# Ordering two off-path steps of a convolution by the scans that run beside it

## The chip, the cores and the metric

The kernel runs on one NeuronCore of one Trainium2 chip. The metric is device time in microseconds (us) of one launch, from its first to its last instruction, as the median of several runs. Engines are named as in the profile: PE is TensorE (PEld its weight loads), DVE is VectorE, ACT is ScalarE, POOL is GpSimd, SP is SyncE, which here only issues DMAs.

## The reference

Four layers run on `x` of shape (4, 128, 64, 64). Only the first two bear on this change; they run together in one function, `layers01`. The other two (linear attention with an expert layer, then windowed attention with an expert layer) follow it and are not touched.

```python
# layer 0, for each image: a selective scan over L = 4096 tokens, 256 channels, 16 states
delta = softplus(dt_r @ dt_proj_w.T + dt_proj_b)
def step(hprev, inp):
    dt_t, B_t, C_t, x_t = inp
    hn = exp(dt_t[:, :, None] * A) * hprev + (dt_t * x_t)[:, :, None] * B_t[:, None, :]
    return hn, einsum('bdn,bn->bd', hn, C_t)

# layer 1, for each image: a hypergraph convolution over the 4096 tokens
incidence = (dist < 16.0)                       # (4096, 4096) zeros and ones
xe = xf @ W_fc.T + b_fc
edge = einsum('bve,bvc->bec', incidence, xe) / deg_e
vert = einsum('bve,bec->bvc', incidence, edge) / deg_v
out = vert + xf
mean, var = over images and tokens, for each channel   # then a batch norm and silu
```

## The kernel before

**Two layers beside each other.** `layer0()` is a generator that yields after every half state. A state is one of the 16 scan states of one chunk of 512 tokens; an image has 8 chunks, so 128 states or 256 half states. `layer1(b, ...)` is a second generator for the convolution of image `b`. The driver first runs image 0 of layer 0 alone and 12 half states of image 1. Then for each of three images it takes 256 half states of layer 0, and after each lets `layer1` go on until the share of its work (costs `W_CMP`, `W_TURN`, `W_EDGE`, `W_VERT` and so on) has caught up. The fourth image of layer 1 runs alone. A counter `tick` grows by one with each half state (in the fourth image, with each yield of `layer1`).

**A state on the engines.** SP loads the rows of B and C, `bt` (L287). POOL makes `db` = `dx` times B (L291, two buffers). ACT makes the decays `hs` with two exponentials (L303, in PSUM, two buffers). DVE scans each half (L309), saves the carry (L318) and multiplies by C into `ho` (L319). In images 1 to 3 POOL adds eight `ho` up (L324, L326) before PE adds the sums in PSUM.

**The convolution.** In the panel phase, PE makes distances (L541) which DVE compares into the 0/1 matrix `inc` (L544); half of the blocks are transposes of others instead (PE L553, ACT L557). `edges` adds up each block of 128 edges with 32 matmuls (L564). Two ticks later `parts` takes the sum on DVE (`ed`, L571), and after the fourth block of a chunk DVE makes the reciprocal degrees `rdeg` (L575, L576), POOL multiplies `ed` by them (L580), ACT copies the product to fp16 as `hi` (L581) and POOL takes the rest `lo` (L582), both in the tensor `es`. In the vertex phase, for each of 8 chunks, PE adds 64 matmuls of `es` and `inc` into `ps_v` (L672). Then `mean` scales the result on DVE (L680, into `rb`, which ACT had filled with the reciprocal degrees of the vertices, L667) and adds the input on POOL (L681); `finish` takes batch statistics on DVE (L684) and stores `rb` by a DMA on SP's queue (L685). The tile `rb` has two buffers, `ps` in PSUM has four.

**What sets the order.** A step that must not come too early is queued by `later(k, f)` and called by `due()` once `tick` has grown by `k`; `due(True)` calls everything at once. `due(True)` runs ahead of the first `edges` of each chunk, and the last chunk's steps are flushed before the vertex phase.

```python
due()
later(1, mean)
later(6, finish)
```

The order in which instructions are written is only a preference. The compiler plans each engine's queue by its own estimate of durations: of the instructions that it takes to be ready, the one written first goes next. So an instruction can be placed ahead of others that were written before it, when the plan thinks the engine idle. Instructions that pass through `act()` are the exception: each gets an order edge to the one before, so ACT's queue here is exactly as written. Once planned, each queue runs in order.

Of the kernel before, what the change touches and what calls it, by code (L numbers as in the profile page):

```python
# [12 lines left out]
ALU = mybir.AluOpType  # L13
# [18 lines left out]
def bc(ap, n):  # L32

    return ap.unsqueeze(1).to_broadcast([ap.shape[0], n, ap.shape[1]])


def bc_last(ap, n):

    return ap.unsqueeze(len(ap.shape)).to_broadcast([*ap.shape, n])


class Net:
# [36 lines left out]
    def layers01(self):  # L79
        nc, tc, a = self.nc, self.tc, self.a  # L80
# [10 lines left out]
        with ExitStack() as ctx:  # L91
# [90 lines left out]
            late = ctx.enter_context(tc.tile_pool(name="late", bufs=1))  # L182


            order = []

            def act(i):


                if order:  # L190
                    tc.add_manual_dep(
                        i.ins, order[-1].name,
                        mybir.DependencyInfo(mybir.DependencyClass.NoSync, mybir.DependencyReason.DATA),
                        reason="order",
                    )
                order[:] = [i.ins]


# [3 lines left out]
            def later(k, f):  # L202
                waiting.append((self.tick + k, f))

            def due(every=False):
                for w in list(waiting):
                    if every or w[0] <= self.tick:
                        waiting.remove(w)
                        w[1]()

            def before(b, c):
# [21 lines left out]
                def conv():  # L233
                    xc = s["xc"] = w2.tile([P, 2, T], F32, tag="xc", name="xc")
                    for h in range(2):
                        act(nc.scalar.activation(xc[:, h, :], s["ps"][h], AF.Silu, bias=vec[:, h, 4:5]))
# [56 lines left out]
            def state(s, n, h):  # L293

                b, c, db = s["b"], s["c"], s["db", n]
                if h == 0:
                    hs = s["hs"] = aps.tile([P, 2, T], F32, tag="hs", name="hs")  # L300
                    s["ho", n] = w2.tile([P, 2, T], F32, tag="ho", name="ho", bufs=6)
                    for k in range(2):
                        act(nc.scalar.activation(hs[:, k, :], s["dl"][:, k, :], AF.Exp, scale=A[:, k, n : n + 1]))  # L303
                hs, ho = s["hs"], s["ho", n]
                ct = bc(s["bt", n][:, 1, :], 2)
                split = b == 0 and n in TO_POOL
                init = 0.0 if c == 0 else carry[:, n, h : h + 1]
                to = ho if split else hs
                nc.vector.tensor_tensor_scan(to[:, h, :], hs[:, h, :], db[:, h, :], init, ALU.mult, ALU.add)  # L309
                if h == 0:  # L310
                    return
                if split:
                    if c < NT - 1:
                        nc.gpsimd.tensor_copy(carry[:, n, :], ho[:, :, T - 1])
                    nc.gpsimd.tensor_tensor(ho, ho, ct, ALU.mult)  # L315
                    return
                if c < NT - 1:
                    nc.vector.tensor_copy(carry[:, n, :], hs[:, :, T - 1])  # L318
                nc.vector.tensor_tensor(ho, hs, ct, ALU.mult)  # L319
                if b == 0 or n % G == 0:  # L320
                    return
                if n % G == 1:
                    s["sum", n // G] = w2.tile([P, 2, T], F32, tag="ho", name="ho_s", bufs=6)
                    nc.gpsimd.tensor_tensor(s["sum", n // G], ho, s["ho", n - 1], ALU.add)  # L324
                else:
                    nc.gpsimd.tensor_tensor(s["sum", n // G], s["sum", n // G], ho, ALU.add)  # L326
# [51 lines left out]
            def layer0():  # L378
# [29 lines left out]
                for i in range(count):  # L408
                    k, n = divmod(i, DS)
                    if i + 3 < count:  # L410
                        rows(*at(i + 3))
                    if i + 1 < count:
                        drive(*at(i + 1))
                    state(*at(i), 0)
                    steps(k, 2 * n)
                    yield
                    state(*at(i), 1)
                    if i > 2:
                        total(*at(i - 3))
                    steps(k, 2 * n + 1)  # L420
                    yield
# [15 lines left out]
            stats = wp.tile([P, B, NCH, 6], F32, tag="stats1", name="stats1")  # L437
# [31 lines left out]
            def layer1(b, rstd, nmr):  # L469
# [89 lines left out]
                def edges(inc, ed, c, i):  # L559


                    pe = ps.tile([P, CH], F32, tag="ps", name="ps_ed")
                    for v in range(NB):
                        nc.tensor.matmul(  # L564
                            pe[:, : 2 * P + 2], inc[:, v, i * P : (i + 1) * P], xs[:, v, :],
                            start=v == 0, stop=v == NB - 1,
                        )

                    def parts():
                        both = pe[:, : 2 * P + 2].rearrange("p (k c) -> p c k", k=2)  # L570
                        nc.vector.reduce_sum(ed[:, i, :], both, axis=AX.X)  # L571
                        if i == 3:

                            rd = rdeg[:, 4 * c : 4 * c + 4]
                            nc.vector.tensor_scalar(rd, ed[:, :, P], 1.0, None, ALU.max)  # L575
                            nc.vector.reciprocal(rd, rd)  # L576
                            e = ed[:, :, :P]
                            hi = es[:, 4 * c : 4 * c + 4, 0, :]
                            lo = es[:, 4 * c : 4 * c + 4, 1, :]
                            nc.gpsimd.tensor_tensor(e, e, bc_last(rd, P), ALU.mult)  # L580
                            later(3, lambda: act(nc.scalar.copy(hi, e)))  # L581
                            later(4, lambda: nc.gpsimd.tensor_tensor(lo, e, hi, ALU.subtract))  # L582

                    later(2, parts)

# [55 lines left out]
                def diagonals(c):  # L641
                    dg = tp.tile([P, 4, P], F32, tag="hb", name="dg")
                    for i in range(4):
                        act(
                            nc.scalar.activation(
                                dg[:, i, :], self.ident, AF.Copy, scale=rdeg[:, 4 * c + i : 4 * c + i + 1]
                            )
                        )
                    return dg
# [4 lines left out]
                for c in range(NCH):  # L654
                    dg = ahead
                    if c < NCH - 1:
                        ahead = diagonals(c + 1)
                    inc = panels[c]
                    if c > 1:
                        inc = tp.tile([P, NB, CH], FP8, tag="inc", name="inc_v")  # L660
                        for q in range(4):
                            nc.sync.dma_start(inc[:, 8 * q : 8 * q + 8, :], panels[c][:, 8 * q : 8 * q + 8, :])

                    pr = ps.tile([P, CH], F32, tag="ps", name="ps_r")
                    nc.tensor.matmul(pr, self.ones, dg.rearrange("p i v -> p (i v)"), start=True, stop=True)
                    rb = tp.tile([P, CH], F32, tag="rb", name="rb")
                    later(1, lambda rb=rb, pr=pr: act(nc.scalar.copy(rb, pr)))  # L667
                    yield W_DEG
                    pv = ps.tile([P, CH], F32, tag="ps", name="ps_v")
                    for e in range(NB):  # L670
                        for k in range(2):
                            nc.tensor.matmul(  # L672
                                pv, es[:, e, k, :], inc[:, e, :],
                                start=e == 0 and k == 0, stop=e == NB - 1 and k == 1,
                            )
                        if e % 4 == 3:
                            yield W_VERT

                    def mean(c=c, rb=rb, pv=pv):
                        nc.vector.scalar_tensor_tensor(rb, pv, top, rb, ALU.mult, ALU.mult)  # L680
                        nc.gpsimd.tensor_tensor(rb, rb, xn[c], ALU.add)  # L681

                    def finish(c=c, rb=rb):
                        nc.vector.bn_stats(stats[:, b, c, :], rb)  # L684
                        nc.sync.dma_start(self.hg[b][:, c * CH : (c + 1) * CH], rb)  # L685

                    due()
                    later(1, mean)
                    later(6, finish)
                while waiting:  # L690
                    due(True)
# [870 lines left out]
```

## Time and profile before

| | |
|---|---|
| median of 3 runs | 4105.99 us (4105.96 to 4106.67) |
| the profiled execution | 4105.69 us, span 4103.9 us |
| busy share of the span | PE 84%, DVE 73%, POOL 60%, ACT 50%, PE weight loads 47% |
| layer 0 of image 0 alone | about 0 to 580 us |
| panel phases beside layer 0 | from about 580, 1347 and 2112 us |
| vertex phases beside layer 0 | from about 1172, 1938 and 2702 us |
| convolution of the fourth image alone | about 2862 to 3310 us |
| layers 2 and 3 | about 3310 us to the end |

A row of the profile names the line of the kernel, the engine, the operation and the tiles it writes and reads (`out<-in`). In a timeline the row begins with its start and its duration in us, and in brackets stands how long its engine was idle before it and what ended that wait. In a table of windows each row holds a stretch of time, its length, the busy time and number of instructions of PE, PEld, DVE, ACT and POOL, and then TensorE's granted clock (1.00 is full speed), the DMA engines' busy share and the GB/s they moved. A row of one line's instructions gives the shortest, median and longest duration in ns. An engine that runs its queue in order passes every wait on to all that stands behind it; what that costs the whole depends on who needs those instructions, and when.

### The profile page before, as it was taken

The numbers are of one execution on the slowest core, as the hardware profiler recorded it, in microseconds if no ns is written. First come the engines' busy times: TensorE is split into PE (matmuls) and PEld (weight loads), VectorE is DVE, ScalarE is ACT, GpSimd is POOL, SyncE is SP. The second block draws the span as 40 slices with busy tenths as digits, with TensorE's granted clock in tenths as the row PEclk, the third lists the DMA queues.
The fourth block names the chain that finished last, engine by engine and source line by source line (L and its number), as shares of the span: only waits on it lengthen the run. The fifth ranks groups of instructions, "written<-read, shape, count | busy, mean of one in ns | idle before, by whom it ended". The sixth has DMA issues, their size and how long they took to land. (4 is left out here: it accounts for less than half of the span.)

```text
span 4103.9 us, 48550 instructions
## 1 busy us (share of the span) xinstructions
PE 3456.7 (84%) x17255; PEld 1931.4 (47%) x17255; DVE 3001.7 (73%) x4628; ACT 2034.9 (50%) x3364; POOL 2460.4 (60%) x1242
## 2 busy tenths in 40 slices
PE   6878767888889788888977888887999979998989
PEld 2323323344543334455433444543567448765864
DVE  5888889999666899975679998664642067665764
ACT  4556554445644555555444455642223158842951
POOL 5998989888678898986879888674100020001300
PEclk8898888899999899999988999999999989999999
DMA  3545544455436454543644455447121420046138
GB/s 101 149 148 155 151 122 126 130 143 152 118 123 199 116 139 130 147 138 87 213 135 130 131 146 145 115 134 246 52 73 55 127 100 11 12 140 218 27 109 298
DMA packets 263845, 532.71 MB, mean 130 GB/s; under 512 B 22794, under 2 KB 25266, under 8 KB 262578
## 3 DMA queue, kind: packets, MB, share of 16 engines
q1 hardware_dynamic: 255666, 519.09, 42.3%
q10 hardware_dynamic: 7936, 10.52, 0.7%
q8 instruction: 136, 2.23, 0.2%
q14 instruction: 107, 0.88, 0.1%
HBM read 451.80 MB, written 77.73 MB: 129 GB/s over the span
## 5 line engine op out<-in xcount | busy, mean ns | idle before, releaser
L291 POOL TENSOR_TENSOR db<-dx,bt 128x1024 f32<-128x1024 f32 x512 | 1202.9, 2352 | 349.5 <-DVE hs L309 204.4
L309 DVE TENSOR_TENSOR_SCAN hs<-hs,carry,db 128x512 f32<-128x512 f32 x812 | 1033.9, 1282 | 257.1 <-ACT hs L303 176.0
L303 ACT ACTIVATE hs<-dl,A 128x512 f32<-128x512 f32 x1024 | 706.0, 692 | 773.1 <-DVE ho L319 721.2
L541 PE MATMUL ps_g<-xn 128*128 128x512 f32 x1152 | 603.5, 654 | 121.3 <-DVE inc L544 95.3
L326 POOL TENSOR_TENSOR ho_s<-ho_s,ho 128x1024 f32<-128x1024 f32 x288 | 677.5, 2352 | 11.7 <-DVE ho L319 6.5
L319 DVE TENSOR_TENSOR ho<-hs,bt 128x1024 f32<-128x1024 f32 x464 | 563.3, 1214 | 1.6
L564 PE MATMUL ps_ed<-xs,inc 128*128 128x258 f16 x4096 | 508.8, 284 | 41.8 <-DVE inc L544 20.2
L564 PEld LDWEIGHTS <-inc 128*128 128x128 fp8e4 x4096 | 414.7, 102 | 160.5 <-issue 88.8
L544 DVE SCALAR_TENSOR_TENSOR inc<-ps_g,hcl,hb 128x512 fp8e4<-128x512 f32 x576 | 418.6, 735 | 26.3 <-PE ps_g L541 12.6
L541 PEld LDWEIGHTS ps_g<-xn 128*128 128x128 f32 x1152 | 214.4, 203 | 439.3 <-DVE inc L544 213.1
L557 ACT CAST inc<-ps_t 128x512 fp8e4<-128x512 f32 x448 | 231.7, 601 | 299.3 <-PE ps_t L553 277.5
L347 PE MATMUL ps_y<-ho,cst 128*128 128x512 f32 x512 | 274.6, 680 | 108.9 <-POOL ho L315 91.5
L672 PE MATMUL ps_v<-inc_v,es 128*128 128x512 fp8e4 x1536 | 344.9, 383 | 18.0 <-DVE rb L680 18.0
L672 PEld LDWEIGHTS <-es 128*128 128x128 f16 x2048 | 203.2, 100 | 287.8 <-issue 65.2
L229 PE MATMUL ps_c<-xt,wc 128*128 128x512 f32 x512 | 234.2, 611 | 4.1 <-DVE inc L544 2.1
L347 PEld LDWEIGHTS ps_y<-ho,cst 128*128 128x128 f32 x512 | 105.5, 215 | 269.0 <-POOL ho L315 121.9
L1231 POOL CAST b1h<-b 128x512 bf16<-128x512 f32 x2 | 1.3, 648 | 302.1 <-DMA b<-in_L_ffn_weight 302.1
L580 POOL TENSOR_TENSOR ed<-ed,rdeg 128x512 f32<-128x512 f32 x32 | 33.2, 1038 | 247.6 <-DVE rdeg L576 247.6
L309 DVE TENSOR_TENSOR_SCAN hs<-hs,db 128x512 f32<-128x512 f32 x116 | 141.3, 1223 | 43.4 <-POOL db L291 36.9
L571 DVE TENSOR_REDUCE ed<-ps_ed 128x129 f32<-128x258 f32 x128 | 52.9, 413 | 159.5 <-PE ps_ed L564 159.5
L229 PEld LDWEIGHTS ps_c<-xt,wc 128*128 128x128 f32 x512 | 99.3, 197 | 127.7 <-issue 114.9
L1467 POOL MEMSET ob<- 128x256 f32 x4 | 1.2, 311 | 262.1 <-PE ps_t L1410 262.1
(317 smaller groups left out, 5463.7 us busy)
## 6 DMA issues: line engine op xcount, KB each, us to landing
bt<-bcd SPq DMA_DIRECT2D x512, 512.0 KB, 4.9
w<-in_L_ffn_weight SPq DMA_DIRECT2D x64, 1024.0 KB, 11.1
inc<-inc SPq DMA_DIRECT2D x192, 256.0 KB, 2.4
inc_v<-inc SPq DMA_DIRECT2D x96, 512.0 KB, 6.4
strip<-inc SPq DMA_DIRECT2D x84, 256.0 KB, 3.0
x<-x ACTq DMA_DIRECT2D x32, 256.0 KB, 5.7
xn<-x SPq DMA_DIRECT2D x32, 256.0 KB, 5.5
hg<-rb SPq DMA_DIRECT2D x32, 256.0 KB, 2.7
```

The source lines that it names most:

```text
L229: nc.tensor.matmul(s["ps"][h], wc[:, h, j, :], xt[:, j : j + T], start=j == 0, stop=j == 3)
L291: nc.gpsimd.tensor_tensor(db, s["dx"], bc(s["bt", n][:, 0, :], 2), ALU.mult)
L303: act(nc.scalar.activation(hs[:, k, :], s["dl"][:, k, :], AF.Exp, scale=A[:, k, n : n + 1]))
L309: nc.vector.tensor_tensor_scan(to[:, h, :], hs[:, h, :], db[:, h, :], init, ALU.mult, ALU.add)
L319: nc.vector.tensor_tensor(ho, hs, ct, ALU.mult)
L326: nc.gpsimd.tensor_tensor(s["sum", n // G], s["sum", n // G], ho, ALU.add)
L347: nc.tensor.matmul(s["y"][h], self.ident, t[:, h, :], start=False, stop=n == DS - 1 and k == len(terms) - 1,)
L541: nc.tensor.matmul(pq, xn[v // 4][:, v % 4 * P : (v % 4 + 1) * P], xn[c], start=True, stop=True)
L544: nc.vector.scalar_tensor_tensor(inc[:, v, :], pq, hc[:, v : v + 1], hb, ALU.subtract, ALU.is_gt, saturate=False)
L557: later(1, lambda: act(nc.scalar.copy(inc[:, v, :], pt, saturate=False)))
L564: nc.tensor.matmul(pe[:, : 2 * P + 2], inc[:, v, i * P : (i + 1) * P], xs[:, v, :], start=v == 0, stop=v == NB - 1,)
L672: nc.tensor.matmul(pv, es[:, e, k, :], inc[:, e, :], start=e == 0 and k == 0, stop=e == NB - 1 and k == 1,)
```

## The change

Two steps of the convolution get another place. The batch statistics of `finish` get an order edge to the scan that was written last when `finish` is called, so the plan can't place them ahead of that scan. And of the products of the edges' sums, ACT's copy is called six ticks after the product instead of three, POOL's subtraction seven instead of four. Durations, shapes and data stay the same; the edge is of the kind that waits for no semaphore.

```diff
+            def follow(i, j):
+                tc.add_manual_dep(
+                    i.ins, j.name,
+                    mybir.DependencyInfo(mybir.DependencyClass.NoSync, mybir.DependencyReason.DATA),
+                    reason="order",
+                )
             order = []
+            scans = []
             def act(i):
                 if order:
-                    tc.add_manual_dep(
...
+                    follow(i, order[-1])
                 order[:] = [i.ins]
...
-                nc.vector.tensor_tensor_scan(to[:, h, :], hs[:, h, :], db[:, h, :], init, ALU.mult, ALU.add)
+                i = nc.vector.tensor_tensor_scan(to[:, h, :], hs[:, h, :], db[:, h, :], init, ALU.mult, ALU.add)
+                scans[:] = [i.ins]
...
                             nc.gpsimd.tensor_tensor(e, e, bc_last(rd, P), ALU.mult)
-                            later(3, lambda: act(nc.scalar.copy(hi, e)))
-                            later(4, lambda: nc.gpsimd.tensor_tensor(lo, e, hi, ALU.subtract))
+                            later(6, lambda: act(nc.scalar.copy(hi, e)))
+                            later(7, lambda: nc.gpsimd.tensor_tensor(lo, e, hi, ALU.subtract))
...
                     def finish(c=c, rb=rb):
-                        nc.vector.bn_stats(stats[:, b, c, :], rb)
+                        follow(nc.vector.bn_stats(stats[:, b, c, :], rb), scans[-1])
                         nc.sync.dma_start(self.hg[b][:, c * CH : (c + 1) * CH], rb)
```

More of the change, by code (lines that the diff above doesn't have):

```diff
@@ L182, in layers01 @@
             late = ctx.enter_context(tc.tile_pool(name="late", bufs=1))
+            def follow(i, j):
[4 more added lines that the diff above has]
+                )
             order = []
+            scans = []
             def act(i):
                 if order:
-                    tc.add_manual_dep(
[L192 to L195, printed above, removed]
+                    follow(i, order[-1])
                 order[:] = [i.ins]
```

## Prediction

> **What bounds the kernel now.** The table of stages (busy time by window) comes first: is one engine the bound while the scans run beside the convolution?
>
> ```profile
> core 0: us, PE busy (x) PEld busy (x) DVE busy (x) ACT busy (x) POOL busy (x), PEclk, DMA share, GB/s
> ...
> 580.00:1172.00 592.00, 488.72 (x2193) 266.27 (x2194) 507.36 (x644) 312.51 (x465) 492.07 (x225) 0.90 0.45 127
> 1172.00:1347.00 175.00, 155.56 (x596) 66.74 (x596) 119.03 (x125) 77.43 (x123) 137.26 (x63) 0.94 0.61 182
> ```
>
> These are an image's panel phase (comparisons and edge sums) and its vertex phase. No engine is full in either: PE, DVE and POOL share the first at 83 to 86%, so a wait costs time where the next engine has no slack; in the second PE is nearest to full (155.6 of 175). This pair runs three times, at 580, 1347 and 2112. Next, the two lines that the change touches.
>
> ```profile
> L684 DVE BATCH_NORM_STATS2 stats<-rb x32: 693/694/696, 1202.9 to 3309.0; 128x6 f32<-128x512 f32 x32
> its engine sat idle before it (us, times) until:
>   POOL rb L681: 119.2, 32
> ...
> L581 ACT CAST es<-ed x32: 617/618/619, 795.8 to 3185.5; 128x512 f16<-128x512 f32 x32
> ...
>   POOL ed L580: 173.6, 31
> ```
>
> Both waits are on POOL, and behind each stands an engine's in-order queue. The timeline shows what one costs (first vertex chunk; the last three PE rows are the first, seventh and, in the third image, sixth chunk):
>
> ```profile
> 1193.31 0.74 DVE L680 SCALAR_TENSOR_TENSOR rb<-ps_v,top,rb 128x512 f32<-128x512 f32 x1
> 1202.93 0.69 DVE L684 BATCH_NORM_STATS2 stats<-rb 128x6 f32<-128x512 f32 x1 [8.88 <-POOL rb L681]
> ...
> 1197.04 2.34 POOL L291 TENSOR_TENSOR db<-dx,bt 128x1024 f32<-128x1024 f32 x1
> 1199.34 2.34 POOL L326 TENSOR_TENSOR ho_s<-ho_s,ho 128x1024 f32<-128x1024 f32 x1
> 1201.64 1.26 POOL L681 TENSOR_TENSOR rb<-rb,xn 128x512 f32<-128x512 f32 x1
> 1206.23 2.35 POOL L291 TENSOR_TENSOR db<-dx,bt 128x1024 f32<-128x1024 f32 x1 [3.33 <-DVE hs L309]
> ...
> 1215.45 2.07 PE L332 MATMUL ps_y<-xc,dD 128*128 128x512 f32 x2 [4.56 <-DVE rb L680]
> ...
> 1321.59 6.62 PE L672 MATMUL ps_v<-inc_v,es 128*128 128x512 fp8e4 x17 [8.63 <-DVE rb L680]
> ...
> 2824.05 2.07 PE L332 MATMUL ps_y<-xc,dD 128*128 128x512 f32 x2 [8.22 <-DVE rb L680]
> ```
>
> DVE runs the statistics straight behind the product L680, although `finish` is emitted five half states after `mean`. It stands 8.88 us for a POOL add that has three 2.34 us instructions before it; then POOL stands 3.33 us for the scans that DVE held back, and PE 4.56 us for the next product. PE has no other wait over 0.3 us between 1232 and 1313, so these few are what DVE's stalls cost. For the copies:
>
> ```profile
> 795.82 0.62 ACT L581 CAST es<-ed 128x512 f16<-128x512 f32 x1 [9.99 <-POOL ed L580]
> ...
> 797.85 1.29 DVE L309 TENSOR_TENSOR_SCAN hs<-hs,carry,db 128x512 f32<-128x512 f32 x1 [4.36 <-ACT hs L303]
> ...
> 799.83 1.22 PE L541 MATMUL ps_g<-xn 128*128 128x512 f32 x1 [4.72 <-DVE inc L544]
> ```
>
> ACT's order is chained by hand: while the copy waits, no exponential behind it runs, the scan is late, then PE.
>
> **The change, part by part.** *Statistics.* No instruction, byte or semaphore is added; 32 instructions of 0.69 us get an order edge. Where do they land? I counted the scans ahead of each instruction in the trace: every L680 stands within one half state of the tick that emits `mean` (scan 210 for tick 209, 216 for 216, ...). `finish` comes at ticks 214, 221, 228, 235, 242, 249, 256, so the statistics move four or five scans back, about two states, or 2 x (2 x 1.29 + 0.15 + 1.21) = 7.9 us of DVE work: as long as the longest wait, 8.89. Not every wait is reached: chunk 7 is flushed with no scan between, the fourth image has no scans left, and in the third the scans end at 244, so its chunks 5 to 7 stay. 18 or 19 of 32 waits should go. Queued behind the statistics on DVE are the scans, and for those wait POOL (`db` buffers) and ACT (`hs`). The store `hg<-rb` (32 of 0.32 us on SP's queue) waits for the add alone and stays; no load is moved.
>
> I retimed the first chunk by its rows. The next scans have their `db` at 1194.8 and 1199.4. POOL, no longer held, starts the row of 1206.23 at 1202.9; the third pair runs from 1205.3, and the product of chunk 1 moves from 1214.66 to about 1209.5. PE was free at 1210.89: its 4.56 go. What is late next is `db`: POOL is the limit there, and keeps 7 us by 1222.86 (3.33 + 0.32 + 3.38).
>
> Behind this wait comes TensorE's clock (the column before the last two):
>
> ```profile
> 1203.00:1210.90 7.90, 7.89 (x33) 3.38 (x31) 7.83 (x9) 2.33 (x6) 4.61 (x2) 1.00 0.60 196
> 1215.40:1221.40 6.00, 5.95 (x7) 2.52 (x8) 1.89 (x2) 0.76 (x2) 4.08 (x3) 0.50 0.75 254
> 1232.00:1310.00 78.00, 77.37 (x310) 33.93 (x311) 51.37 (x50) 37.17 (x57) 64.19 (x31) 1.00 0.70 209
> ```
>
> After the wait 6.0 us ran at 0.50, so 3.0 were lost. The Trainium skill (TensorE: Matmul & The Clock Gate, Part 1) says that an idle window of about 3.4 us halves the clock and a busy one of that length restores it: 1.7 us lost. I take the row's 3.0; by the rule the sum is 4 us smaller over three images. So chunk 0: 4.56 + 3.0 = 7.6, three times = 22.8.
>
> Wait at 1321.59 (images one and two): POOL is gapless from 1266 to 1305, so nothing is won there; behind it the `db` of 1308.74 comes 3.2 sooner and that of 1312.22 4.3, and the product of 1320.80 at about 1316.3. 4.5 of 8.63 go, and the rest still halves the clock: 2 x 4.5 = 9.0. In the third image PE stands 8.22 us, and the window after it loses 2.5. Three POOL gaps of 3.3 to 3.8 us after DVE's stalls, with 5.5 between the last two products, cover that: 10.7.
>
> A rule against it: by the Trainium skill (SBUF — State Buffer, Who interferes with whom), a VectorE instruction with two SBUF inputs, or in a two-port mode, and a GpSimd one lock each other out for a whole instruction. The moved scans now run on top of POOL's backlog; if locked, they would end no sooner, and these 42.5 us were nil. The trace has POOL's product at 2332/2352/2391 ns over 512 instructions, beside an idle and a busy DVE alike: the scan reads `hs` from PSUM. The lock is seen only on L575 (155 to 2153 ns), which isn't moved. I take nil cost.
>
> *Copies.* Ticks of the copies, worked out from the yields: chunks 7 to 3 and 1 go three half states later; chunk 2 one, since the flush at the second strip catches it; chunk 0 is flushed as before. In time three half states are 3 x 764.6/256 = 9.0 us. Chunk 7: ACT is free at 785.8, POOL's product ends at 795.8; the wait goes, the exponentials run, and the scan starts at DVE's own 793.5 instead of 797.85. Its `db` was ready at 787.74. Here PE waits for DVE, so 4.1 x 3 = 12.3. Chunk 2: the 1.15 us behind it, 3.5. Chunk 1 (8.85 of ACT, 4.79 of DVE): PE is busy without a break from 1133 to 1162, nil. Others: ACT waits of 0 to 4 us and no scan late behind them, nil. Cost: chunk 1's subtraction (1.1 us) now comes just ahead of chunk 0's product on POOL, for which PE waits 8.04 us at 1171.76; POOL has gaps of 2.5 and 1.3 us there, so nil to 1.1 each, and I take 1.1: +3.3.
>
> Sum: -22.8 - 9.0 - 10.7 - 12.3 - 3.5 + 3.3 = **-55.0** against the profiled execution's 4105.69 (span 4103.9): 4050.7. The median of the runs, 4105.99, lies 0.3 higher: **4051**.
>
> What the trace can't show is the order that the compiler's planner writes anew. Nearest row: image three, with other work beside it, repeats image one's waits on chunks 0 to 2 to 0.02 us and differs later by 2 to 5. I let it cost or bring 20.
>
> **The rivals.** *POOL takes the place (22%).* If the planner puts one sum (2.35) ahead of the `db` that scans need, each wait on the add returns by that much: 3 x 2.2 + 2 x 2.1 + 3.5, no clock won, with 12.5 of the copies: -27, 4079. For: POOL is 78% busy there. Against: its gaps follow DVE's stalls.
>
> *ACT takes the place: slower (13%).* `rb` has two buffers. ACT's copy L667 of chunk c+2 can't write before the statistics of chunk c have read, and all exponentials stand behind it. Statistics at tick 214, copy at 216: two scans and a product, 3.9 us, against copy and two exponentials, 2.0. That is 1.9 us of slack; if the statistics land two scans later than their tick, it is gone. Then each wait on the add comes back through ACT, with 2.0 on top: 18 x 2.0 = +36, copies -12.5: 4129. Against: the trace keeps L680 and L667 within one half state of their ticks.
>
> *It does nothing (7%).* The named scan could already stand ahead of the product, as at the image's end; then 4105, less what copies bring.
>
> **How the numbers follow.** Main case 58%, own range 4020 to 4080. 0.2% is 8 us, about what a measurement tells from no change. Faster: main and POOL, 0.80; same 0.07; slower 0.13. The range 4015 to 4110 leaves out ACT's case and a gain beyond 90 us, for which all PE waits of the vertex phases and all late scans behind copies would have to vanish.
>
> **What would show it.** The wait of L684 falls from 119.2 to about 20, that of L581 from 173.6 to about 90; PE's waits for L680 at a vertex phase's first chunk vanish with their half-clock windows; `DVE hs <- POOL db` (86.6) grows; each of the three periods of 764.6 us shortens by about 18. Wrong: L667 or L309 waiting more for ACT, or the statistics' wait gone and PE's unchanged.

## The result, and the profile after

| | before | after |
|---|---|---|
| median | 4105.98 us (4102.38 to 4106.67, 4 runs) | 4049.03 us (4046.74 to 4054.35, 4 runs) |
| profiled execution, span | 4105.69 us, 4103.9 us | 4054.35 us, 4052.6 us |

The ratio is 0.9865, with a 95% interval of 0.9848 to 0.9882: 57 us by the medians, 51 by the two profiled executions. The profiled execution of after is the slowest of its four, so sums over its trace come out some 5 us short of the medians. The lines of the code have moved: what was L309 (scan) is L314, L291 (`db`) L296, L580 (product of the sums) L586, L581 (copy) L587, L667 (copy into `rb`) L673, L672 (`ps_v`) L678, L680 (product into `rb`) L686, L681 (add) L687, L684 (statistics) L691.

First the vertex window that answers to the forecast's second row, then the row of the statistics, then three rows of the list of waits (us, times, longest), all of after:

```profile
1170.00:1328.00 158.00, 150.31 (x596) 65.65 (x596) 115.65 (x124) 78.10 (x124) 137.20 (x64) 0.98 0.67 200
```

```profile
L691 DVE BATCH_NORM_STATS2 stats<-rb x32: 665/674/695, 1201.4 to 3257.4; 128x6 f32<-128x512 f32 x32
...
  POOL rb L687: 20.7, 13
```

```profile
DVE hs L314 <- ACT hs L308: 203.2, 64, 9.4
...
DVE hs L314 <- POOL db L296: 112.2, 67, 26.0
...
ACT es L587 <- POOL ed L586: 72.2, 13, 13.7
```

and the scans' two waits in before:

```profile
DVE hs L309 <- ACT hs L303: 180.9, 66, 9.4
...
DVE hs L309 <- POOL db L291: 86.6, 50, 26.1
```

The same 596 matmuls fit into 158 us instead of 175. PE is busy for 150.3 us of them instead of 155.6, since its clock is 0.98 instead of 0.94; it idles 7.7 instead of 19.4. The wait of the statistics is 20.7 us in 13 times (119.2 in 32 before), the copy's 72.2 in 13 (173.6 in 31), and the scans wait longer: for `db` 112.2 instead of 86.6, for ACT's decays 203.2 instead of 180.9.

Where did the 51 us come from? An image is cut where PE begins its row norms (first `ps_hb`), and where it begins the degrees of the first vertex chunk (first `ps_r`). These are differences of start times in the two traces:

| us | image 1 | image 2 | image 3 | together |
|---|---|---|---|---|
| panel phase, before | 590.6 | 585.3 | 585.2 | 1761.1 |
| panel phase, after | 589.0 | 583.5 | 589.9 | 1762.4 |
| vertex phase, before | 179.3 | 179.4 | 174.7 | 533.4 |
| vertex phase, after | 162.3 | 163.8 | 154.3 | 480.3 |

All of it lies in the vertex phases (53.1 us), where the statistics are, and none in the panel phases, where the copies are. The first image's vertex phase in detail: PE's timeline of after, then tables of windows, of after (the place of the first wait, then behind the wait that is left) and of before (behind the last chunk's wait).

```profile
1206.20 1.89 PE L678 MATMUL ps_v<-inc_v,es 128*128 128x512 fp8e4 x8 [0.44 <-DMA inc_v<-inc]
1207.93 1.88 PE L338 MATMUL ps_y<-xc,dD 128*128 128x512 f32 x4
1209.64 3.60 PE L353 MATMUL ps_y<-ho_s,cst 128*128 128x512 f32 x8
...
1301.48 1.02 PE L671 MATMUL ps_r<-dg,ones 128*128 128x512 f32 x2
1305.88 6.38 PE L678 MATMUL ps_v<-inc_v,es 128*128 128x512 fp8e4 x21 [3.37 <-DVE rb L686]
```

```profile
1206.20:1213.00 6.80, 6.80 (x20) 3.06 (x20) 6.65 (x7) 1.38 (x2) 6.80 (x4) 1.00 0.96 286
...
1306.70:1310.10 3.40, 3.40 (x9) 1.21 (x8) 3.37 (x4) 0.00 (x0) 3.40 (x2) 0.50 0.62 227
1310.10:1323.50 13.40, 13.40 (x58) 6.38 (x57) 6.90 (x14) 3.76 (x4) 11.62 (x6) 1.00 0.62 158
```

```profile
1321.60:1327.20 5.60, 5.60 (x14) 2.02 (x14) 0.00 (x0) 0.70 (x2) 5.60 (x3) 0.50 0.31 99
1327.20:1330.60 3.40, 3.40 (x17) 1.50 (x16) 3.23 (x5) 0.00 (x0) 0.10 (x1) 0.99 0.52 154
```

PE goes from the first chunk into `ps_y` L338 without a wait; the 4.56 us and the half clock behind them are gone. The wait of 8.63 us before the last chunk is 3.37, and the clock behind it is halved for 3.4 us instead of 5.6. In the third image the wait of 8.22 us is gone too. How this came about is in DVE's timeline of after, behind the product of the first chunk:

```profile
1191.75 0.74 DVE L686 SCALAR_TENSOR_TENSOR rb<-ps_v,top,rb 128x512 f32<-128x512 f32 x1
1193.26 2.62 DVE L314 TENSOR_TENSOR_SCAN hs<-hs,carry,db 128x512 f32<-128x512 f32 x2 [0.77 <-POOL db L296]
1197.86 1.29 DVE L314 TENSOR_TENSOR_SCAN hs<-hs,carry,db 128x512 f32<-128x512 f32 x1 [1.99 <-POOL db L296]
...
1201.43 0.67 DVE L691 BATCH_NORM_STATS2 stats<-rb 128x6 f32<-128x512 f32 x1
```

Four scans now run between product and statistics, and they wait 0.77 and 1.99 us for `db`: of the wait of 8.88 us some 6 are gone, and 2.76 have passed on to the scans.

### The profile page after: what moved, and what is told of

It is laid out like the page before. It is cut to its first block, busy times and chain, and to the rows that moved or that the text cites. A ratio compares the mean times of both kernels' runs of the same rounds, so it can differ in the third digit from the quotient of the medians.

```text
span 4052.6 us, 48609 instructions
## 1 busy us (share of the span) xinstructions
PE 3443.5 (85%) x17255; PEld 1930.0 (48%) x17255; DVE 2995.6 (74%) x4628; ACT 2035.6 (50%) x3364; POOL 2460.9 (61%) x1242
## 5 line engine op out<-in xcount | busy, mean ns | idle before, releaser
L296 POOL TENSOR_TENSOR db<-dx,bt 128x1024 f32<-128x1024 f32 x512 | 1203.9, 2355 | 291.2 <-DVE hs L314 159.7
L314 DVE TENSOR_TENSOR_SCAN hs<-hs,carry,db 128x512 f32<-128x512 f32 x812 | 1034.5, 1282 | 293.7 <-ACT hs L308 198.2
L678 PE MATMUL ps_v<-inc_v,es 128*128 128x512 fp8e4 x1536 | 344.0, 383 | 8.9 <-DVE rb L686 7.3
L678 PEld LDWEIGHTS <-es 128*128 128x128 f16 x2048 | 202.9, 99 | 277.2 <-issue 53.6
L586 POOL TENSOR_TENSOR ed<-ed,rdeg 128x512 f32<-128x512 f32 x32 | 33.3, 1040 | 245.9 <-DVE rdeg L582 245.9
L314 DVE TENSOR_TENSOR_SCAN hs<-hs,db 128x512 f32<-128x512 f32 x116 | 141.3, 1224 | 49.4 <-POOL db L296 42.8
L577 DVE TENSOR_REDUCE ed<-ps_ed 128x129 f32<-128x258 f32 x128 | 52.9, 413 | 157.6 <-PE ps_ed L570 157.6
```

The costliest lines, as they stand in the source:

```text
L296: nc.gpsimd.tensor_tensor(db, s["dx"], bc(s["bt", n][:, 0, :], 2), ALU.mult)
L314: i = nc.vector.tensor_tensor_scan(to[:, h, :], hs[:, h, :], db[:, h, :], init, ALU.mult, ALU.add)
L678: nc.tensor.matmul(pv, es[:, e, k, :], inc[:, e, :], start=e == 0 and k == 0, stop=e == NB - 1 and k == 1,)
```

## Experiments

Each edit is made to the kernel before or after as its diff says. Ratios are to the kernel before on the same chip (its medians there were 4102.0 to 4103.2 us).

**1. Which half of the change is it?** The edge alone, then the copies alone.

```diff
 # edge alone, against after
-later(6, lambda: act(nc.scalar.copy(hi, e)))
-later(7, lambda: nc.gpsimd.tensor_tensor(lo, e, hi, ALU.subtract))
+later(3, lambda: act(nc.scalar.copy(hi, e)))
+later(4, lambda: nc.gpsimd.tensor_tensor(lo, e, hi, ALU.subtract))
 # copies alone, against before: the same two lines, from 3 and 4 to 6 and 7
```

> The order edge of the statistics alone; the copies stand at three and four half states as before. Theory A (the gain is all in the vertex phases, where the trace after the change shows -17.0, -15.7 and -20.4 us against before): about 4106 - 53 = 4053. Theory B (the parts add up as predicted, statistics 42.5 and copies 12.5): about 4063. L684's wait falls to about 20 us in both.

> The later copies alone; the statistics stand where the plan puts them. Theory A (after chunk 7's copy the scan pair waits for db on POOL instead, so nothing is left at the panel phase's end): 4106, within 4 us either way, although the copies' wait for POOL falls by about 100 us. Theory B (as predicted, 4.1 us for chunk 7 and 1.15 for chunk 2 in each image, less 1.1): 4093.5.

Edge alone: 4049.46 us, ratio 0.9872 (0.9858 to 0.9885). Copies alone: 4099.78 us, ratio 0.9989 (0.9982 to 0.9995). So the edge is worth 53 us of the 55 that the ratio of after stands for, and the copies 4.5 alone (2 to 7.5), and at most a few us on top of the edge. In the two traces the edge alone leaves the order of PE's, ACT's and POOL's instructions as it was; on DVE, apart from the statistics, three neighbouring pairs have changed places. So what the forecast could not see, a queue planned anew, hardly happened. The copies' profiled execution, the fastest of its 21 (4092.36), shows panel phases that are 11.8 us shorter together, the one of after 1.3 us longer: single traces scatter here by more than the effect, and the ratios decide. Yet the copies' edit does to its wait what it does in after, and leaves the other alone. The waits of the copies alone:

```profile
ACT es L581 <- POOL ed L580: 72.2, 13, 13.7
...
DVE stats L684 <- POOL rb L681: 119.2, 32, 8.9
```

A hundred us of a wait gone, and 4.5 us of time: this needs a cause (experiment 5).

**2. How far behind must the statistics stand?** With the edge alone, `finish` three or eight ticks after `mean` is queued instead of six.

```diff
-later(6, finish)
+later(3, finish)     # and, in another kernel, later(8, finish)
```

> The order edge alone, with finish called three ticks after the chunk instead of six, so the statistics stand one or two scans behind the product instead of four or five. Theory A (the edge gains as much as the scans cover of the wait for POOL's add): 2.6 to 3.9 us of cover against waits of up to 8.9, so the waits of 8.9, 8.2, 5.8 and 6.9 us leave 4 to 6 each, PE keeps a good part of its waits and its half-clock windows: about 4085. Theory C (any place behind a scan is enough, since DVE then no longer stands ahead of work that is ready): about 4053, as with the full distance.

> The order edge alone, with finish called eight ticks after the chunk instead of six: the statistics of chunk c then come in the same tick as ACT's copy into the same rb buffer for chunk c+2. Theory of the rival on ACT (the copy waits for the statistics, the exponentials stand behind it, 2.0 us of copy and exponentials come back in each of 18 places[...]): slower than the edge at six ticks by 20 to 36 us, about 4080, with L673 waiting for DVE. Theory A (DVE has slack of a state there, because scans wait for db anyway): within 5 us of the edge at six ticks.

Three ticks: 4083.82 us, ratio 0.9955 (0.9941 to 0.9968). Eight: 4057.97 us, ratio 0.9890 (0.9876 to 0.9903). Their lists of waits, three ticks first:

```profile
DVE stats L691 <- POOL rb L687: 69.7, 25, 6.8
```

```profile
ACT rb L673 <- PE ps_r L671: 153.4, 20, 19.3
ACT rb L673 <- DVE stats L691: 38.2, 9, 5.2
```

With three ticks 69.7 us of the wait are left, and PE stands 6.50 us before the last chunk of image 1. The gain follows the wait: its vertex phases take 171.3, 171.7 and 164.4 us, halfway between before and after. With eight ticks the wait that the forecast's slower rival named appears: ACT's copy into `rb` waits 38.2 us for statistics that read the buffer late. But it hardly reaches PE: the vertex phases take 162.5, 163.9 and 153.8 us, against 162.2, 162.2 and 153.9 of the edge alone. The rival's mechanism is real, and its price was wrong by far. (The 8.5 us are also more than the 5 of the other theory, though the intervals of the two kernels overlap.) The 8.5 us that this kernel is slower lie mostly in the panel phases by the two traces, where PE's windows of the first image, of the edge alone and then of the eight ticks, read:

```profile
582.00:1170.00 588.00, 481.32 (x2193) 262.06 (x2193) 507.32 (x644) 312.15 (x463) 492.03 (x225) 0.91 0.49 128
```

```profile
582.00:1170.00 588.00, 488.21 (x2192) 266.76 (x2192) 506.88 (x644) 310.33 (x457) 491.00 (x224) 0.90 0.50 128
```

The two kernels have the same instructions in the same order in PE's queue, yet PE is busy 6.9 us longer here, at a lower clock. Why this kernel falls on the worse side in all its runs (4055.4 to 4059.9) stays open.

**3. Is it the wait for POOL's add?** The add goes to DVE, ahead of the statistics on the same engine: first in the kernel before, without any edge; then with the edge alone.

```diff
-nc.gpsimd.tensor_tensor(rb, rb, xn[c], ALU.add)
+nc.vector.tensor_tensor(rb, rb, xn[c], ALU.add)
```

> Neither part of the change. The add of the input to rb is taken from POOL and put on DVE, straight behind the product L680, so that the statistics can't wait for POOL. Theory A (the wait for POOL's add, with what it holds up, is all that the order edge removes): DVE pays 32 adds of about 0.7 us where it has slack, PE loses the same waits as with the edge: about 4050 to 4060. Theory D (the trace only names the add; DVE must wait there for POOL's backlog anyway, since the scans need db): about 4100, the wait standing at L309 for POOL instead. By the shared-port rule the add has two SBUF inputs and so can stand for a POOL instruction of 2.35 us: durations well over 0.7 us would show it.

> The order edge of the statistics, with the add on DVE as in the run before. Theory A: with no wait on POOL's add there is nothing for the edge to remove: the same as the add on DVE alone, within 4 us. Theory C (the gain comes from where the statistics stand, not from the wait): faster than the add on DVE alone by 30 us or more.

Without the edge 4049.38 us, ratio 0.9868 (0.9853 to 0.9883); with it 4049.21 us, ratio 0.9866 (0.9850 to 0.9883). No wait at the statistics is left in the first, and its vertex phases take 162.4, 162.5 and 154.8 us. Taking the wait away in another way gives the change's gain, and the edge then adds nothing. By itself this doesn't clear POOL's load, since the add (1.26 us) leaves POOL's queue too; but with the edge POOL keeps every add, and in experiment 2 the gain follows the wait. So the wait was the cause. The edit also costs DVE the add, whose row in the first of them is

```profile
L681 DVE TENSOR_TENSOR rb<-rb,xn x32: 691/1248/2869, 1190.9 to 3250.0; 128x512 f32<-128x512 f32 x32
```

1.25 us in the median, from 0.69 to 2.87 for one shape; the eight of image 1 come to 14.4 us. The vertex phases have that time to spare on DVE: they take as long as with the edge alone.

**4. What bounds the vertex phase next?** In after PE still stands before the first chunk, between the last panel's work and `ps_r` (PE's timeline of after):

```profile
1160.17 1.98 PE L258 MATMUL ps_d<-xd,dtT 8*128 8x512 f32 x4
1170.20 2.07 PE L671 MATMUL ps_r<-dg,ones 128*128 128x512 f32 x2 [8.05 <-ACT dg L651]
```

The chain is chunk 0's product on POOL, ACT's copy, then the diagonals `dg`. But of the 64 matmuls of the first vertex chunk only eight need chunk 0's sums, and they may come last. So the first vertex chunk takes the edge blocks 8 to 31 first, then 4 to 7 and 0 to 3, and the flush, the diagonals and `ps_r` come after the 24th block. The second kernel is the first with the copies at three and four ticks again.

```diff
-while waiting: due(True)            # ahead of the vertex phase
-ahead = diagonals(0)
...
-for e in range(NB):
+turns = list(range(NB)) if c > 0 else [*range(8, NB), *range(4, 8), *range(4)]
+for m, e in enumerate(turns):
+    if c == 0 and m == NB - 8:
+        while waiting: due(True)
+        dg = diagonals(0); ahead = diagonals(1); rb = degrees(dg)
```

> The changed kernel, and the vertex phase begins with the edges of chunks 2 to 7; those of chunks 1 and 0, the flush of the copies and the reciprocal degrees of the first chunk come after three quarters of its matmuls. It aims at the wait that the change left alone: PE 8.05 us at the start of each vertex phase, ACT 9.86 us for POOL's product of chunk 0. Theory A (waits that PE meets with nothing else to do cost their length and the half clock behind them): 8 + 1.7 in three images and some 4 in the fourth, about 4049 - 33 = 4016. Theory F (ACT's chained queue only meets the same POOL product later): PE's wait goes, but DVE's 9.4 us for the exponentials stay: about 4035.

> As the run before, with the copies at three and four half states as before the change. Theory A (the later copies are worth 0 to 4 us, as the copies alone gave 0.9989 and nothing on top of the edge): within 5 us of the run before. Theory B (they are worth the 12.5 us of the prediction once the wait at the start of the vertex phase no longer hides them): 12 us slower than the run before.

4022.67 us, ratio 0.9801 (0.9787 to 0.9816), the fastest kernel of this study that leaves nothing out, and faster than both before and after; with the early copies 4027.43 us, ratio 0.9812 (0.9798 to 0.9827). PE's timeline of the first:

```profile
1157.91 1.98 PE L258 MATMUL ps_d<-xd,dtT 8*128 8x512 f32 x4
1159.82 10.53 PE L690 MATMUL ps_v<-inc,es 128*128 128x512 fp8e4 x48
1170.19 1.02 PE L671 MATMUL ps_r<-dg,ones 128*128 128x512 f32 x2
```

PE has work through what was the gap. The result lies between the two theories (4016 and 4035); the scans' wait for the decays, which the second expected to stay, fell from 203.2 to 170.1 us. The copies' place makes 4.8 us again, with intervals that overlap: the same small size as in experiment 1.

**5. Why are the copies worth so little?** Four kernels. First the product of the sums moves to DVE, so that ACT's copy can come soon after it, without POOL's queue: with the edge alone, and with experiment 4's first kernel.

```diff
-nc.gpsimd.tensor_tensor(e, e, bc_last(rd, P), ALU.mult)
+nc.vector.tensor_tensor(e, e, bc_last(rd, P), ALU.mult)
```

> The order edge alone (copies at three and four half states), and the product of the edges' sums with the reciprocal degrees is taken from POOL and put on DVE, behind the reciprocal. ACT's copy then waits for POOL nowhere, and POOL is relieved of 32 products of 1.04 us; DVE gets 32 of 0.7 us or, where POOL holds the shared port, up to 2.9. Theory A (in the panel phase ACT's waits for the product lie beside waits for db and for TensorE, so taking them away by any means brings next to nothing there; only chunk 0, for which PE waits, gains some 2.3 us of POOL's backlog and 1 of its product in each image): 4049 - 10 = 4039, within 5. Theory B (the waits of chunks 7 and 2 were worth 12 to 16 us and the later copies lost it again by standing elsewhere): 4049 - 10 - 14 = 4025.

> The version with the chunks 1 and 0 last in the first vertex chunk and later copies, and the product on DVE. Theory A: chunk 0 no longer holds PE, so the product's place is worth nothing more: within 4 us of that version's 4022.7. Theory B: faster by 5 us or more, since POOL, which bounds the scans, is relieved of 1.04 us in 24 places.

4067.10 us, ratio 0.9916 (0.9903 to 0.9930), and 4052.91 us, ratio 0.9883 (0.9869 to 0.9897): slower than the same kernels without the edit by 18 and 30 us by the medians, which no theory had. The product's rows, of the one and of the other:

```profile
L586 DVE TENSOR_TENSOR ed<-ed,rdeg x32: 676/693/2707, 787.0 to 3142.4; 128x512 f32<-128x512 f32 x32
```

```profile
L586 DVE TENSOR_TENSOR ed<-ed,rdeg x32: 674/1864/2828, 789.5 to 3148.3; 128x512 f32<-128x512 f32 x32
```

In the fourth image, where no scan and no `db` runs, all eight take 0.69 us; beside POOL's work up to 2.83. In the first kernel an image's eight products come to 13.4 us (summed over its rows), 40 in three images, and the medians differ by 18. In the second they come to about 15 us, 45 in three images; its panel phases are longer by 15.1, 10.8 and 11.7 us than without the edit in the profiled executions (of this kernel the slowest of four), and the medians differ by 30. So much of what is put on DVE there comes out at the end (18 of 40 us, 30 of 45), though ACT's wait gets shorter (134.1 us instead of 175.4 in the first kernel). In before DVE is busy for 86% of the panel phase and 68% of the vertex phase, which fits with experiment 3. PE's and ACT's queues are the same with and without the edit; DVE's and POOL's are planned anew, and that part of the loss was not taken apart.

Then two kernels in which the copy no longer waits for the product. In the first the product is left out and the copy reads the degrees; in the second the product stays and only its readers go. Both leave the edges' sums out of the result.

```diff
 # against the edge alone; the first also drops the product
-later(3, lambda: act(nc.scalar.copy(hi, e)))
-later(4, lambda: nc.gpsimd.tensor_tensor(lo, e, hi, ALU.subtract))
+later(3, lambda: act(nc.scalar.copy(hi, bc_last(rd, P))))
+later(4, lambda: nc.gpsimd.tensor_tensor(lo, bc_last(rd, P), hi, ALU.subtract))
```

> The edge alone, and of the edges' sums the product is left out: ACT's copy and POOL's subtraction read the reciprocal degrees, spread over the tile, instead of the product, with the same shapes. This leaves the scaling and the sums themselves out of the result. It takes away all that a later copy could ever win in the panel phases: ACT waits for POOL's product nowhere (175.4 us before), and POOL has 32 instructions of 1.04 us less. Theory of the forecast (the copies' waits cost PE 12.5 us over three images): at least 12 us faster than the edge alone, about 4037 or less. Theory A (POOL's queue of 2.35 us instructions without a gap, and PE's other waits, set the pace of the panel phases; the copies' waits lie beside them): within 6 us of the edge alone, 4044 to 4056.

> The edge alone, and ACT's copy and POOL's subtraction read the reciprocal degrees, spread over the tile, instead of the product; the product itself stays on POOL, and nothing reads it. This leaves the edges' sums out of the result. Against the run without the product it gives POOL its 32 instructions of 1.04 us back, so that what is left out is the wait of ACT's copy for them alone (175.4 us in the edge alone). From an image's first ps_hb matmul to its last ps_ed matmul the edge alone takes 577.2, 575.1 and 575.1 us, the run without the product 573.2, 570.0 and 574.7. Theory of the forecast (the wait is what costs PE): these three together shorten by 9 us or more, as without the product or better. Theory A (POOL's queue has no gap there, so its work counts and not the wait): they shorten by 5 us or less. The stretch from the last ps_ed to the first ps_r, 10.2 us in the edge alone, should fall to about 7 by either, since the copy that it waits for no longer stands behind the product. The whole: about 4030 by the forecast, 4035 to 4041 by A.

4026.65 us, ratio 0.9814 (0.9800 to 0.9827), and 4022.19 us, ratio 0.9806 (0.9793 to 0.9820): more than theory A allowed, and at first sight the forecast's theory is right. The stretches that the second expectation names separate it (in the second kernel PE and DVE keep the very order of the edge alone):

| us | first `ps_hb` to last `ps_ed` | last `ps_ed` to `ps_r` |
|---|---|---|
| edge alone | 577.2, 575.1, 575.1 | 10.2, three times |
| no product | 573.2, 570.0, 574.7 | 6.8, three times |
| product without a reader | 577.0, 571.6, 571.6 | 6.8, three times |

Of 17.5 us that the second gains there, 10.2 lie in the gap of experiment 4, which a later copy doesn't touch: it is flushed at once, and the gap is 10.2 us in after as in before. In the panel phases 7.3 us are left (0.2, 3.5 and 3.5), between the bounds that the two theories had set; for the first kernel theory A had overlooked the gap. But this is no upper bound for the copies. ACT still waits there, now for the degrees (list of waits of the second kernel):

```profile
ACT es L587 <- DVE rdeg L582: 97.9, 23, 13.7
```

For chunks 7 to 1 of an image that is 14.0 us, against 33.9 with the edge alone and 0.9 in after: the later copies take away more. And the medians lie 27 us apart where the two traces lie 20, so the panel phases' share may be larger than 7.3. What the later copies are worth is measured by experiment 1.

The place of chunk 7's copy shows why. POOL's timeline there, before:

```profile
794.75 1.04 POOL L580 TENSOR_TENSOR ed<-ed,rdeg 128x512 f32<-128x512 f32 x1
796.51 1.12 POOL L582 TENSOR_TENSOR es<-ed,es 128x512 f16<-128x512 f32 x1 [0.73 <-ACT es L581]
797.58 2.35 POOL L291 TENSOR_TENSOR db<-dx,bt 128x1024 f32<-128x1024 f32 x1
799.88 2.36 POOL L326 TENSOR_TENSOR ho_s<-ho_s,ho 128x1024 f32<-128x1024 f32 x1
802.19 2.35 POOL L291 TENSOR_TENSOR db<-dx,bt 128x1024 f32<-128x1024 f32 x1
```

and after, with DVE and PE:

```profile
794.64 1.05 POOL L586 TENSOR_TENSOR ed<-ed,rdeg 128x512 f32<-128x512 f32 x1
795.64 2.36 POOL L296 TENSOR_TENSOR db<-dx,bt 128x1024 f32<-128x1024 f32 x1
797.95 2.35 POOL L332 TENSOR_TENSOR ho_s<-ho_s,ho 128x1024 f32<-128x1024 f32 x1
800.26 1.13 POOL L588 TENSOR_TENSOR es<-ed,es 128x512 f16<-128x512 f32 x1
801.33 2.35 POOL L296 TENSOR_TENSOR db<-dx,bt 128x1024 f32<-128x1024 f32 x1
```

```profile
803.72 1.29 DVE L314 TENSOR_TENSOR_SCAN hs<-hs,carry,db 128x512 f32<-128x512 f32 x1 [2.44 <-POOL db L296]
...
806.10 0.42 DVE L577 TENSOR_REDUCE ed<-ps_ed 128x129 f32<-128x258 f32 x1
```

```profile
806.67 5.33 PE L547 MATMUL ps_g<-xn 128*128 128x512 f32 x6 [5.40 <-DVE ed L577]
```

The scan behind the copy does start 4.5 us earlier (793.32 instead of 797.85). But from 780.8 to 812 POOL's queue has no gap in after, and before only the one of 0.73 us: its second `db` after the product moves from 802.19 to 801.33. The third pair of scans, which needs it, waits 2.44 us, the sum `ed` L577 comes at 806.10 instead of 808.11, and PE, which waited 4.72 and 1.90 us here, waits 5.40 for that one. Of 4.5 us 2.0 are left; the kernel with no reader of the product also gains 2.0 over this place (against the edge alone its compares before it are 2.7 us late, the sum 0.7). The step is the same everywhere: between the fourth and the fifth sum `ed` of a phase, after and the copies alone gain 1.9 us on before in all three images. It does not last. In image 1 nothing of it is left at the 24th of the 32 sums (1091.36 us in after, 1091.32 in before); behind chunk 2's copy some comes back, and at the end of the phase (last `ps_ed`) it is 1.6 us. In image 3, counted from the phase's start, after is 4.3 us behind before already at the fourth sum, ahead of any copy, so its longer panel phase is not the copies' doing.

## Why the prediction was right, and where it was off

The forecast of 4051 stands 2 us from the median of 4049.03. Its terms don't stand so well: two errors of some 10 us cancel, so that the closeness is luck.

- **The statistics, sized 42.5, are worth 53** (the vertex phases; the edge alone, 4106 x 0.0128 = 53). Its mechanism is shown: experiment 3 removes the wait otherwise and gets the same, and experiment 2 leaves part of the wait and gets part. Chunk 0's 7.6 us came nearly as worked out: up to the last chunk's `ps_r`, image 1 gains 1311.94 - 1301.48 = 10.5 us, less 1.6 that it brought along, so 8.9.
- **The term of it that was mis-sized most is the second wait (1321.59), 4.5 us; in image 1 8.1 came.** PE's wait fell by 8.63 - 3.37 = 5.3, and the forecast left the halved clock behind it at its old price. The halved stretch behind it shrank from 5.6 to 3.4 us, which is another 1.1; from `ps_r` to the next image the sum is 17.0 - 8.9 = 8.1, of which 1.7 are not traced to a row. In the third image 18.3 were forecast (10.7 and chunk 0's 7.6) and 20.4 came.
- **Cost of the moved scans: nil, as taken.** No lock on POOL's products shows where scans now run beside them (at most 2.39 us each, as before). The lock shows on DVE instructions with two tiles in SBUF, as the Trainium skill (SBUF — State Buffer, Who interferes with whom) has it: 691/1248/2869 ns for the add and up to 2828 for the product, in experiments 3 and 5.
- **The copies, sized 15.8 (12.5 after their cost), brought 4.5 alone** and 0 to 3 on top of the edge. The step that failed is "Its `db` was ready at 787.74. Here PE waits for DVE": true of the first pair of scans, not of the third. Chunk 7 was to bring 4.1 us an image; 1.9 came at its place, and they did not last. I followed the freed wait to its first waiter and stopped, two pairs of scans short of the next bound, which was POOL's full queue. I had applied that question to the statistics ("what is late next is `db`") and not here.
- **The cost of chunk 1's subtraction, +3.3, didn't come.** The gap before chunk 0's vertex work is 8.05 us in after, 8.04 before.
- **The signs named came:** 20.7 us (said: about 20), 72.2 (said: 90), PE's waits for the product at the first chunks gone, the scans' wait for `db` grown. The periods shortened by 18.6, 17.5 and 15.7 us (said: about 18). One sign that was to show the forecast wrong came as well: the scans wait more for ACT's decays, 24.2 us instead of 13.2 in each of the first two vertex phases, and more for `db`, 9.0 instead of 3.1. So of the 35.5 us of the statistics' wait that are gone from each of these phases about 17 stand at the scans instead, and PE still gains 15.7 to 17.0: the sign was badly chosen.
- **The rivals.** POOL takes the place: in part, with some 6 us more of waiting for `db` in a vertex phase, and with most of what the copies were to bring. ACT takes the place: not at this distance; one or two half states further, its wait is there (38.2 us) and costs PE's vertex phases next to nothing. It does nothing: excluded.

## What to carry to other kernels

An instruction that nobody waits for still holds an in-order queue: put it behind the work that can run while its own input is made, and no further than its buffer allows. When a wait is taken away, follow the freed time through the second and third instruction of every engine that it passes, until one has no gap in its queue; here that engine's own gap (0.73 us) was nearer to the gain (2.0) than the length of the wait (9.99). Before work is moved to another engine, ask whether that engine has slack in that phase: DVE took eight adds in the vertex phase for nothing, and eight products in the panel phase at a loss.

## What the runs showed of the hardware that I had not expected

- The duration of a DVE instruction with two tiles in SBUF beside a busy POOL is spread by a factor of four: 674 to 2828 ns for one product, 0.69 us where no `db` runs beside it. POOL pays as well, more rarely: with the add on DVE (experiment 3, without the edge) 17 of its instructions that take 2.35 us elsewhere take 2.8, where in before and after none takes over 2.45.
- Equal PE queues take unequal time: PE is busy for 481.3 us at a granted clock of 0.91 and 488.2 at 0.90 in the first panel phase of two kernels whose PE queues are the same, and panel phases take between 583.5 and 589.9 us in one execution of after. Why the clock differs was not found out. A few us in a single trace's panel phase are therefore no finding; the medians over several runs, or a wait traced through its rows, are.
